# Gated scan and top-2 mixture of experts on one core: one PSUM-bank step in each pump call, and both input transposes of the next expert in one set

## The chip, the cores and the metric

The kernel runs on one core of a Trainium2 chip. The metric is the device time of one execution in microseconds (us). Beside the plain runs there is one profiled execution, whose trace gives the start and length of every instruction on five engines: PE (TensorE matmul, with PEld for its weight loads), DVE (VectorE), ACT (ScalarE), POOL (GpSimd) and SP (SyncE, which only issues DMAs).

## What is computed

The input has 8 groups of 1024 tokens with 256 channels, all float32. There are two layers, each behind a layernorm and with a residual.

```
h    = rmsnorm(layernorm(x)) * gamma
q, kv, a = split(h @ w_qkva.T)                 # 256 channels each
y_t  = sigmoid(a_t) * y_(t-1) + kv_t           # a scan over the 1024 tokens of a group
x    = x + q * y
z    = layernorm(x)
for each token: the two best of 8 experts by softmax(z @ router_w),
    at most 256 tokens of a group per expert (CAP), the gates are the softmax values
expert e: (gelu(z @ w0[e]) * (z @ w1[e])) @ wo[e]     # 256 -> 1368 -> 256
out  = x + sum over the token's experts of gate * expert output
```

## The kernel before, in words

**Blocks.** The 8 groups are worked in four blocks n = 0 to 3 of two groups. The token work (scan layer, router, gates) of a block runs in units u of 512 tokens, four to a block. The expert work of a block is 8 experts e, each with 2 x 256 gathered token rows. An expert's hidden width of 1368 is cut into six sets s = 0 to 5 of 256 columns (the last has 88), so a block has 48 sets and the program has 192. While PE multiplies the experts of block n, the token work of block n+2 is woven between the products.

**A set (`run_set`, L880).** The two-by-two block products are done in Strassen's manner, seven products in place of eight, with sums of weights made on POOL (`row_sums`, `out_sums`) and sums of inputs on DVE. A product is four matmuls of 256 columns. Four products add up one after the other in one bank z, and ACT copies z out after the first, second and third (the snapshots `snap0`, `snap1`, `snap2` at L913, L927, L934). The fourth, `st.mm(z, a22, t4, False)` at L947, may only write z when the third snapshot has been taken. Between these products stand second-layer products of earlier sets (`products()`, with a hand-written list of shares by set: set 1 has none between the third and the fourth z product), and two calls of `pump()`: the first between the third and the fourth z product (L943), the second at the set's end (L961). The engines' queues follow the order in which the program is written (`tc.manual_schedule`): nothing is reordered.

**PSUM.** There are eight banks: y0 to y3 hold the experts' output sums, z0 and z1 alternate as z of a set, `pb` is a third product bank, and `aside` is for everything else. In a set with bank z0, the bank z1 first takes the product `p_a` (L918), which DVE reads soon after; from then until the next set takes it as its z it is free, and is called `spare`. All work that is not an expert product takes its bank from `ps_a` (L69), which goes round the list `side`:

```
side[:] = ["aside", spare]
pump()
side[:] = [spare]
```

A bank is one buffer: the next use of it waits until the last one has been read by ACT or DVE.

**The work between.** A pump call runs the closures that a planner (L1038 to L1062) put into it. The token work is a list of steps in fixed order, each with a weight (`weigh`, L197), and the planner puts steps into call k of 88 until their weights reach an even share of the sum; what doesn't fit goes to call 88 (the block has 96). A step "with a bank" is one in which PE writes a bank for ACT or DVE to read: `h_channels` and `x_channels` (four transposes, L192, then an ACT copy), `gate_a`, `scan` and `mix` (a projection, L257, read by ACT, by the DVE scan, by a DVE multiply), `to_tokens` (transposes L290, a DVE add), `router` (L327), `positions` and `tokens` (L415 and L506). The other steps are DVE work: layernorm moments, row scaling, softmax, one-hot rows, and so on.

**`between()`** (L1092) does the expert's own side work by set: the transposes of the next expert's gathered rows (`input_channels`, L671: two halves k, four transposes each, an ACT copy each) in sets 1 and 3, or in 3 and 4 for the first expert of a block and for the second of block 0; and in sets 2 and 5 the transposes of the previous expert's outputs (`output_rows`, L863, an ACT copy, a DMA to DRAM). In set 1 it runs in front of the fourth z product, in every other set behind it. `column_sums` (DVE, sets 4 and 5) then makes the sums of the next expert's inputs. In set 1 DVE also joins the previous expert's output sums (`join_outputs`).

Of the kernel before, what the change touches and what calls it, by code (L numbers as in the profile page):

```python
# [17 lines left out]
def kernel(  # L18
# [15 lines left out]
    KC = D // P  # L34
# [159 lines left out]
            )  # L194
        nc.scalar.copy(dst[:, k, :], pt)

    def weigh(w, f):  # L197

        f.weight = w
        return f  # L200

    mid_front = []
# [3 lines left out]
    def unit_steps(u, ps):  # L206
# [127 lines left out]
                pl[:, : UT * NE],  # L334
            )

        def each(w, f):
            return [weigh(w, lambda c=c: f(c)) for c in range(2)]

        pause = [weigh(0, lambda: None)]  # L340
        before_mixer = each(12, first_moments) + each(12, first_norm) + pause
        before_mixer += each(3, h_channels)
        mixer = [f for fs in zip(each(5, gate_a), each(13, scan), each(7, mix)) for f in fs]
        mixer += pause + each(7, to_tokens)
        after_mixer = each(12, second_moments) + each(10, second_norm) + pause
        after_mixer += each(3, x_channels)
        after_mixer.append(weigh(3, router))
        return before_mixer, mixer, after_mixer

    def gate_steps(n):  # L350
# [148 lines left out]
        def tokens(gl):  # L499
            tn = v["tn"]  # L500
            ptok = ps_a(f"ptok_{n}_{gl}")
            for q in range(2 * TPG):
                r, j = divmod(q, TPG)
                at = hot.pop((gl, q))
                for hh in range(NH):
                    nc.tensor.matmul(  # L506
                        ptok[:, hh * 2 * NE : (hh + 1) * 2 * NE],
                        lhsT=at[:, hh * P : (hh + 1) * P],
                        rhs=tn[:, r, gl * TPG + j].rearrange("p k e -> p (k e)"),
                        start=(q == 0 and hh == 0), stop=True, skip_group_check=True,  # L510
                    )
            pk = ptok[:, : NH * 2 * NE].rearrange("p (h k e) -> p h k e", h=NH, k=2)
            td = pg.tile([P, NH, NE], FP, tag="td", name=f"td_{n}_{gl}")
            V.tensor_scalar(td, pk[:, :, 0, :], float(P), None, ALU.mult)
            V.tensor_tensor(tok[n][:, gl], td, pk[:, :, 1, :], ALU.add)
# [1 line left out]
        steps = [weigh(12, softmax), weigh(9, softmax_sum)]  # L517
        steps += [weigh(10, lambda r=r, q=q: top(r, q)) for r in range(2) for q in range(2)]
        steps += [weigh(13, lambda q=q: counts(q)) for q in range(2)]
        steps += [weigh(7, positions), weigh(9, places), weigh(9, kept),  # L520
                  weigh(6, output_places), weigh(20, slot_tokens)]
        for gl in range(GB):
            steps += [weigh(13, lambda gl=gl, q=q: one_hot(gl, q)) for q in range(4)]
            steps.append(weigh(6, lambda gl=gl: tokens(gl)))
        return steps

    def combine_steps(n):
# [137 lines left out]
    def input_channels(n, e, k):  # L665

        if k == 0:
            cols[n, e] = pb.tile([P, KC, GB, CAP], FP, tag="xT", name=f"xT_{n}_{e}")
        pt = ps_a(f"px_{n}_{e}_{k}")
        for q in range(UT):  # L670
            nc.tensor.transpose(  # L671
                pt[:, q * P : (q + 1) * P], inputs[n, e][q][:, k * P : (k + 1) * P], ident
            )
        nc.scalar.copy(cols[n, e][:, k, :, :].rearrange("p g s -> p (g s)"), pt)
# [205 lines left out]
    def run_set(j, last, due, pump, between):  # L880


        V, A = nc.vector, nc.scalar
        st = Set(j)
        a11, a12, a22, s1, s2, s3, s4 = st.a
        b11, b21, b22, t1, t2, t3, t4 = st.b
        nm = f"{st.n}_{st.e}_{st.s}"
        z, p_b = bank(f"z{j % 2}", f"z_{nm}"), bank("pb", f"pb_{nm}")
        st.pb = p_b
        st.hid = pb.tile([P, GB, 2, CAP], FP, tag="hid", name=f"hid_{nm}", bufs=3)  # L890
        st.h2 = st.hid.rearrange("p g c s -> p g (c s)")
        zz = st.cut(z)
        work = [f for o in due for f in out_work(o)]
        summed = last and last.s < NS - 1 and not plain(last.n, last.e)
        joined = units[units.index((st.n, st.e)) - 1] if st.s == 1 and j > NS else None
        if joined and plain(*joined):
            joined = None
        if st.s == 1:
            shares = [1, 2, 1, 0, 0]
        elif len(due) > 1:  # L900
            shares = [1, 1, 2, 2, 2]
        elif due and plain(due[0].n, due[0].e):
            shares = [1, 0, 1, 1, 1]
        else:
            shares = [0, 2, 1, 3, 1] if st.s == 2 else [2, 0, 1, 3, 1]

        def products():
            for _ in range(min(len(work), shares.pop(0))):
                work.pop(0)()

        st.mm(z, a11, b11, True)
        snap0 = st.ten("snap", "sn0", 4)
        A.copy(snap0, zz)  # L913
        if last:
            first_gate(last)
        products()
        spare = f"z{1 - j % 2}"
        p_a = bank(spare, f"pa_{nm}")  # L918
        st.mm(p_a, a12, b21, True)
        c11 = st.ten("cg", "c11", 3)  # L920
        V.tensor_tensor(c11, snap0, st.cut(p_a), ALU.add)  # L921
        if last:
            second_gate(last)
        products()
        st.mm(z, s2, t2, False)
        st.snap1 = st.ten("snap", "sn1", 4)
        A.copy(st.snap1, zz)  # L927
        if joined:
            join_outputs(*joined, 0)
        products()  # L930
        st.mm(p_b, s1, t1, True)
        st.mm(z, s3, t3, False)
        snap2 = st.ten("snap", "sn2", 4)
        A.copy(snap2, zz)  # L934
        A.activation(c11, c11, AF.Gelu_apprx_tanh)
        V.tensor_tensor(st.h2[: st.hs, 1, st.wide], snap2, st.cut(p_b), ALU.add)  # L936
        if joined:
            join_outputs(*joined, 1)
        elif summed:
            hid_sums(last, 0)  # L940
        products()
        side[:] = ["aside", spare]
        pump()  # L943
        side[:] = [spare]
        if st.s == 1:
            between()
        st.mm(z, a22, t4, False)  # L947
        V.tensor_tensor(st.h2[: st.hs, 0, st.wide], zz, c11, ALU.mult)  # L948
        if joined:
            join_outputs(*joined, 2)  # L950
        if st.s != 1:
            between()
        side[:] = ["aside"]
        products()
        st.mm(p_b, s4, b22, False)
        first_sum(st)
        if joined:
            hid_sums(last, 0)
        if summed:
            hid_sums(last, 1)  # L960
        pump()  # L961
        return st
# [73 lines left out]
    with tc.manual_schedule():  # L1036
        last, pending, late = None, [], [[] for _ in range(UB)]
        for n in range(NB):  # L1038
# [12 lines left out]
            if n + 1 < NB:  # L1051
                steps = list(token_work[n + 2])
                share = (sum(f.weight for f in steps) + sum(load[: PUMPS - 8])) / (PUMPS - 8)
                done = 0.0
                for k in range(PUMPS - 8):
                    done += load[k]
                    while steps and done + steps[0].weight / 2 <= share * (k + 1):
                        done += steps[0].weight
                        at_pump(k, steps.pop(0))
                for f in steps:  # L1060
                    at_pump(PUMPS - 8, f)
                at_pump(PUMPS - 7, lambda n=n: gather_unit(n + 1, 0))  # L1062
# [12 lines left out]
            def pump():  # L1075
                for f in plan.pop(at[0], []):
                    f()
                j, half = at[0] // 2 + n * NE * NS, at[0] % 2
                e, s = at[0] // (2 * NS), j % NS
                nxt = (n, e + 1) if e + 1 < NE else (n + 1, 0)  # L1080
                later = (n, e + 2) if e + 2 < NE else (n + 1, 1)
                if half == 0:
                    if j == 0:
                        gather_unit(0, 1)
                    if s == NS - 1 and e + 2 != NE and later in units:
                        gather_unit(*later)
                if nxt in units:
                    if s == (4, 5)[1 - half]:
                        column_sums(*nxt, 1 - half)
                at[0] += 1  # L1090

            def between():  # L1092
                q = at[0] // 2
                e, s = q // NS, q % NS
                nxt = (n, e + 1) if e + 1 < NE else (n + 1, 0)

                slots = (3, 4) if nxt[1] == 0 or nxt == units[1] else (1, 3)
                if s in slots and nxt in units:
                    input_channels(*nxt, slots.index(s))
                before = (n, e - 1) if e > 0 else (n - 1, NE - 1)  # L1100
                if s in (2, 5) and before in yts:
                    output_rows(*before, s // 5)
                    if s == 5:
                        yts.pop(before)
# [50 lines left out]
```

## Time and profile before

| | |
|---|---|
| median of 3 runs | 2044.55 us (2042.69 to 2045.44) |
| the profiled execution, own time | 2044.96 us |
| its span, first to last instruction | 2043.1 us |
| PE busy | 1986.1 us (97%), 9352 matmuls |
| PE weight loads busy | 1633.9 us (80%) |
| DVE, POOL, ACT busy | 1360.0, 1236.5, 685.6 us |
| the expert work's first set starts | 140.0 us after the span's start |

The profiled execution lies 0.41 us above the median, and its span 1.9 us below its own time. Matmuls are pipelined: one of 256 columns is listed with some 380 ns, and the next starts 216 ns after it. So an idle time that the profile lists before a matmul begins only when the listed end has passed, and the stream of starts was by then some 165 ns late.

### The profile page before, as it was taken

Reading aid. Unit: us, or ns where it says so; the run is one execution under the profiler, and the core shown is the slowest. Engines: PE = TensorE matmul, PEld = TensorE weight load, DVE = VectorE, ACT = ScalarE, POOL = GpSimd, SP = SyncE. Lnnn points to the kernel's source line nnn. Section 1 sums busy time; section 2 is a strip of 40 time slices with the busy share of each in tenths; the row PEclk is TensorE's granted clock in tenths of the full one; section 3 lists DMA queues with packets and bytes.
Section 4 is the critical chain, followed back from the end, with each engine's and each line's share of the span. In section 5 each row is a group of like instructions: output and inputs, shape, how many; then the busy total and the mean of one; then the engine's idle time right before and its main releaser. Section 6 shows DMA issues by size and latency. Waiting matters only on the chain.

```text
span 2043.1 us, 27788 instructions
## 1 busy us (share of the span) xinstructions
PE 1986.1 (97%) x9352; PEld 1633.9 (80%) x9352; DVE 1360.0 (67%) x2617; ACT 685.6 (34%) x1286; POOL 1236.5 (61%) x1754
## 2 busy tenths in 40 slices
PE   8889999999999999999999999999999999999999
PEld 4557777888888778788888878888888888888887
DVE  4466565676866575768776666677876677666645
ACT  3233333333333233333333333334333333333332
POOL 2327465545656565767665666666756677677557
PEclk9789999999999999999999999999999999999999
DMA  5223333323323334443424343444434343443453
GB/s 175 73 75 98 91 99 93 107 83 102 108 77 108 116 88 132 119 147 109 133 81 117 109 119 93 140 130 120 124 102 114 104 124 110 129 136 107 123 169 96
DMA packets 224077, 228.87 MB, mean 112 GB/s; under 512 B 32448, under 2 KB 215744, under 8 KB 223936
## 3 DMA queue, kind: packets, MB, share of 16 engines
q1 hardware_dynamic: 211104, 193.51, 32.1%
q0 software_dynamic: 12288, 33.57, 5.5%
q8 instruction: 76, 1.25, 0.3%
q14 instruction: 65, 0.53, 0.1%
q10 hardware_dynamic: 544, 0.01, 0.0%
HBM read 185.61 MB, written 41.42 MB: 111 GB/s over the span
## 4 chain that ended last, share of the span: by engine, by line
PE 91%; DVE 4%; POOL 2%; ACT 2%; issue 1%; DMA 1%; SPq 0%; DVEq 0%; ACTq 0%; POOLq 0%
PE z L745 30%; PE acc L797 24%; PE pb L745 15%; PE pa L745 7%; PE pa L257 3%; PE pkv L257 2%; PE pq L257 2%; PE py L777 2%; PE pl L327 1%; PE pt_y L863 1%; PE px L671 1%; PE po L290 1%; ACT sn L934 1%; PE pt_h L192 1%; PE pt_x L192 0%
## 5 line engine op out<-in xcount | busy, mean ns | idle before, releaser
L701 POOL TENSOR_TENSOR sb<-w 128x256 f32<-128x256 f32 x188 | 130.1, 692 | 418.3 <-PE pb L745 417.5
L745 PE MATMUL z<-tb,sb 128*128 128x256 f32 (+1 forms) x1408 | 368.2, 380 | 0.0
L936 DVE TENSOR_TENSOR hid<-sn,pb 128x512 f32<-128x512 f32 x192 | 123.0, 641 | 270.7 <-ACT sn L934 270.7
L745 PEld LDWEIGHTS z<-tb,sb 128*128 128x128 f32 (+1 forms) x1408 | 264.3, 188 | 42.0 <-issue 0.6
L913 ACT COPY sn<-z 128x512 f32<-128x512 f32 x192 | 105.6, 550 | 396.4 <-PE z L745 396.4
L797 PE MATMUL acc<-hid,wo 128*128 128x256 f32 x840 | 222.5, 382 | 0.0
L797 PE MATMUL acc<-tw,so 128*128 128x256 f32 x900 | 218.7, 379 | 0.0
L921 DVE TENSOR_TENSOR c<-sn,pa 128x512 f32<-128x512 f32 x192 | 122.2, 637 | 125.8 <-PE pa L745 123.6
L934 ACT COPY sn<-z 128x512 f32<-128x512 f32 x192 | 105.6, 550 | 277.9 <-PE z L745 277.9
L745 PE MATMUL z<-tb,w 128*128 128x256 f32 (+1 forms) x704 | 187.6, 385 | 9.4 <-ACT sn L934 9.4
L927 ACT COPY sn<-z 128x512 f32<-128x512 f32 x192 | 105.6, 550 | 269.0 <-PE z L745 268.9
L797 PEld LDWEIGHTS acc<-tw,so 128*128 128x128 f32 x900 | 171.0, 190 | 24.2
L745 PE MATMUL z<-xT,w 128*128 128x256 f32 (+1 forms) x704 | 187.9, 386 | 0.0
L745 PE MATMUL pa<-xT,w 128*128 128x256 f32 (+1 forms) x704 | 186.9, 385 | 0.5 <-DVE hid L948 0.4
L745 PE MATMUL pb<-xT,sb 128*128 128x256 f32 (+1 forms) x704 | 184.5, 381 | 0.0
L745 PE MATMUL pb<-tb,sb 128*128 128x256 f32 (+1 forms) x704 | 183.5, 379 | 0.0
L797 PEld LDWEIGHTS acc<-hid,wo 128*128 128x128 f32 x840 | 160.9, 192 | 23.4
L871 DVE TENSOR_TENSOR c<-sn,pb 128x512 f32<-128x512 f32 x192 | 122.7, 639 | 75.1 <-PE pb L745 74.0
L745 PEld LDWEIGHTS z<-tb,w 128*128 128x128 f32 (+1 forms) x704 | 126.7, 187 | 46.8 <-ACT sn L934 17.7
L745 PEld LDWEIGHTS z<-xT,w 128*128 128x128 f32 (+1 forms) x704 | 130.0, 190 | 32.7 <-issue 11.6
L704 POOL TENSOR_TENSOR sb<-w,sb 128x256 f32<-128x256 f32 x188 | 155.2, 825 | 0.0
L658 POOL DMA_INDIRECT xg<-xn,tok x128 | 127.9, 1000 | 39.1 <-issue 31.9
(176 smaller groups left out, 3788.6 us busy)
## 6 DMA issues: line engine op xcount, KB each, us to landing
w<-in_L_ffn_w_kernel_dram SPq DMA_DIRECT2D x320, 256.0 KB
wo<-in_L_ffn_wo_kernel_dram SPq DMA_DIRECT2D x160, 256.0 KB
y<-ot SPq DMA_DIRECT2D x62, 256.0 KB
xt<-in_L_attn_x_dram SPq DMA_DIRECT2D x16, 512.0 KB
x<-xt SPq DMA_DIRECT2D x16, 512.0 KB
xn<-xn SPq DMA_DIRECT2D x16, 512.0 KB
xc<-x SPq DMA_DIRECT2D x16, 512.0 KB
out_dram<-xc SPq DMA_DIRECT2D x12, 512.0 KB
```

The lines of the kernel that those rows point to most:

```text
L257: nc.tensor.matmul(pp, lhsT=wT[:, k, c * P : (c + 1) * P], rhs=t["hT"][:, k, :], start=(k == 0), stop=(k == KC - 1),)
L658: nc.gpsimd.indirect_dma_start(out=xg, out_offset=None, in_=xn_d[n * GB + gl][:, :], in_offset=bass.IndirectOffsetOnAxis(ap=tok[n][:, gl, ...
L701: eng.tensor_tensor(s1, a21, a22, ALU.add)
L704: eng.tensor_tensor(s4, a12, s2, ALU.subtract)
L745: nc.tensor.matmul(ps[:hs, i * CAP : (i + 1) * CAP], lhsT=a[:, i * hs : (i + 1) * hs], rhs=b, start=first and i == 0, stop=True, skip_grou ...
L797: nc.tensor.matmul(ys[n, e, i][:, half * CAP : (half + 1) * CAP], lhsT=lhsT, rhs=rhs, start=fresh, stop=True, skip_group_check=True,)
L871: nc.vector.tensor_tensor(st.c12, st.snap1, st.cut(st.pb), ALU.add)
L913: A.copy(snap0, zz)
L921: V.tensor_tensor(c11, snap0, st.cut(p_a), ALU.add)
L927: A.copy(st.snap1, zz)
L934: A.copy(snap2, zz)
L936: V.tensor_tensor(st.h2[: st.hs, 1, st.wide], snap2, st.cut(p_b), ALU.add)
```

## The change

The planner is told which steps need a bank (`banks`, a second argument of `weigh`), and puts at most one of them into a pump call; when a second one is due, the call is closed, and that step and all behind it go to the next. The weights of these steps become 6 where they were 3 or 5. Both halves of the next expert's input transposes are made in set 1 (the exception keeps sets 3 and 4). `between()` stands in front of the fourth z product in every set. The banks go round differently: the step in the first pump call takes `spare` first, and `between()` takes `aside` first and then `spare`. No instruction is added or removed.

```diff
-    def weigh(w, f):
+    def weigh(w, f, banks=0):
-        f.weight = w
+        f.weight, f.banks = w, banks
...
-        before_mixer += each(3, h_channels)
-        mixer = [f for fs in zip(each(5, gate_a), each(13, scan), each(7, mix)) for f in fs]
-        mixer += pause + each(7, to_tokens)
+        before_mixer += each(6, h_channels, 1)
+        mixer = [f for fs in zip(each(6, gate_a, 1), each(13, scan, 1), each(7, mix, 1)) for f in fs]
+        mixer += pause + each(7, to_tokens, 1)
...
-        after_mixer += each(3, x_channels)
-        after_mixer.append(weigh(3, router))
+        after_mixer += each(6, x_channels, 1)
+        after_mixer.append(weigh(6, router, 1))
...
-        steps += [weigh(7, positions), weigh(9, places), weigh(9, kept),
+        steps += [weigh(7, positions, 1), weigh(9, places), weigh(9, kept),
...
-            steps.append(weigh(6, lambda gl=gl: tokens(gl)))
+            steps.append(weigh(6, lambda gl=gl: tokens(gl), 1))
...
         products()
+        side[:] = [spare, "aside"]
+        pump()
         side[:] = ["aside", spare]
-        pump()
-        side[:] = [spare]
-        if st.s == 1:
-            between()
+        between()
+        side[:] = ["aside"]
         st.mm(z, a22, t4, False)
         V.tensor_tensor(st.h2[: st.hs, 0, st.wide], zz, c11, ALU.mult)
         if joined:
             join_outputs(*joined, 2)
-        if st.s != 1:
-            between()
-        side[:] = ["aside"]
         products()
...
                     done += load[k]
+                    free = 1
                     while steps and done + steps[0].weight / 2 <= share * (k + 1):
+                        free -= steps[0].banks
+                        if free < 0:
+                            break
                         done += steps[0].weight
                         at_pump(k, steps.pop(0))
...
-                slots = (3, 4) if nxt[1] == 0 or nxt == units[1] else (1, 3)
-                if s in slots and nxt in units:
-                    input_channels(*nxt, slots.index(s))
+                slots = (3, 4) if nxt[1] == 0 or nxt == units[1] else (1, 1)
+                if nxt in units:
+                    for k in range(KC):
+                        if s == slots[k]:
+                            input_channels(*nxt, k)
```

## The prediction

> **What bounds the kernel now.** I read the page first: busy times, the clock in slices, the chain that ended last.
>
> ```profile
> PE 1986.1 (97%) x9352; PEld 1633.9 (80%) x9352; DVE 1360.0 (67%) x2617; ACT 685.6 (34%) x1286; POOL 1236.5 (61%) x1754
> ...
> PEclk9789999999999999999999999999999999999999
> ...
> PE 91%; DVE 4%; POOL 2%; ACT 2%; issue 1%; DMA 1%; SPq 0%; DVEq 0%; ACTq 0%; POOLq 0%
> ```
>
> PE carries the chain from end to end. The change adds and removes no matmul, so all that can move is time in which PE stands still or runs slowly. I therefore asked for PE's own waits after 140 us, where the expert sets start; what comes before isn't touched.
>
> ```profile
> PE z L745 <- ACT sn L934: 9.4, 26, 0.7
> PE ptok L506 <- DVE oneh L496: 3.1, 4, 2.1
> PE pt_x L192 <- DVE oT L284: 2.9, 3, 1.1
> PE pt_h L192 <- ACT xnT L195: 2.3, 4, 0.7
> PE po L290 <- ACT xnT L195: 1.6, 3, 0.7
> ...
> PE po L290 <- ACT logits L332: 1.4, 5, 0.3
> PE pt_x L192 <- ACT hT L195: 1.4, 2, 0.7
> ```
>
> Two kinds. The first row is the fourth z product waiting for the third snapshot. Most of the rest are steps with a bank waiting until an earlier step's bank has been read (a transpose into `pt_x` doesn't need `oT`: it needs the bank that the multiply into `oT` was reading). The timelines of PE show one of each, set 1 of an expert and a pump call with four bank steps:
>
> ```profile
> 722.20 1.03 PE L745 MATMUL z<-tb,sb 128*128 128x256 f32 x4
> 723.07 0.60 PE L671 MATMUL px<-ident,xg 128*128 128x128 f32 x4
> 723.96 1.13 PE L745 MATMUL z<-tb,w 128*128 128x256 f32 x4 [0.29 <-ACT sn L934]
> ```
>
> ```profile
> 693.32 1.88 PE L257 MATMUL pq<-hT,wT 128*128 128x512 f32 x4
> 696.26 0.66 PE L192 MATMUL pt_x<-ident,xn 128*128 128x128 f32 x4 [1.07 <-DVE oT L284]
> 697.60 0.66 PE L192 MATMUL pt_h<-ident,h 128*128 128x128 f32 x4 [0.68 <-ACT xnT L195]
> 698.93 1.11 PE L192 MATMUL pt_x<-ident,xn 128*128 128x128 f32 x4 [0.68 <-ACT hT L195]
> 699.84 1.91 PE L745 MATMUL z<-xT,w 128*128 128x256 f32 x4
> ```
>
> The last row is stretched: four matmuls that elsewhere take 1.03 us take 1.91. The windows view (third number from the end: the granted clock) says why.
>
> ```profile
> 695.10:698.50 3.40, 1.41 (x9) 0.83 (x8) 1.07 (x3) 0.80 (x2) 2.77 (x4) 1.00 0.90 266
> 698.50:701.90 3.40, 2.97 (x9) 2.58 (x10) 0.00 (x0) 1.08 (x3) 3.17 (x5) 0.50 0.77 267
> ```
>
> **What the skill says.** The Trainium skill, "Perfetto Trace Analysis", Matmuls, wants independent groups to go round different banks so that emptying one overlaps the next group; the rows above are places where that fails. "PSUM — Partial Sum Buffer", PSUM bank collisions, has a bank guarded as a whole, which is why any reader of it holds the next writer. "TensorE: Matmul & The Clock Gate", Part 1, says that the clock is judged in free-running windows of 3413 ns and goes to half after an idle one. The trace agrees on length (after 140 us, stretches at half clock of 3.41, 3.41, 3.41, 6.83 and 3.41 us, at 316, 699, 712, 801 and 1511 us) but not on "idle"[...]. Four of the five follow calls with several bank steps, the fifth a wait of `ptok`.
>
> **The change, part by part.** A wait costs more than its listed idle time: the start stream is 0.165 us late when idle begins (380 minus 216 ns), and the matmul behind the restart comes 0.10 us late (0.055 for a transpose), as starts in the trace show.
>
> *One bank step in a call.* I worked the planner's loop through by its weights. Before, 25 calls hold 68 bank steps, so 43 steps stand behind another in one call. After, all 55, 55 and 30 bank steps of the three lists find calls of their own, none is left for call 88. In the waits list, rows of that kind (all with L192, L257, L290, L327, L863 waiting) sum to 14.5 us in 27 waits: 14.5 + 27 x 0.22 = **20.4 us gone**. A lone first-call step reads its bank back before the next set's z product wants `spare`: that product comes exactly where a second-call step stood when `aside` was reused, and of the nine cases of that in the trace with one step in each of the two calls none waited. What is late next: a DVE step in front of a bank step in a first call (about 5 calls), 0.5 us in all, from 0 to 3.
>
> *Slow clock.* 20.5 us at half speed lost 10.2. Without the piles I expect one new stretch, 1.7: **8.5 gone**; ends 3 and 10.2.
>
> *Set 1.* It has 27 experts with transposes there. Before, 21 wait 0.29 + 0.165 + 0.104 = 0.56 us, three (with a step in the call) 0.13: 12.2. With eight transposes (8 x 0.109 = 0.87) in front, the snapshot, ready 0.89 after the third product, leaves 0.02 + 0.10. That holds where the first call has no bank step: 14 x 0.125 = 1.75. In the other 13 the step takes `spare`, the first half `aside`, and the second half needs `spare` again: it waits for the step's reader. Say T is the end of the third z product. From the set at 723.07: ACT copies the snapshot at T + 0.25, has gelu to do, and its next copy ends at T + 1.84; so five calls with an ACT reader (one `hT`, one `xnT`, three transposes of block 3) wait from T + 0.87 to T + 1.9: 1.07 with restart. DVE does two 0.6 us operations first and begins the step's at T + 2.07 (set at 782.41): an add of 0.69 (`to_tokens`, two calls) 2.0 us, a multiply behind a projection of 1.72 (one call) 0.7, a scan of 1.25 (three) 1.3, a router (two) 0.15. Sum 5.35 + 4.0 + 0.7 + 3.9 + 0.3 = 14.3. Set 1 after: 16.0, **3.8 worse**. Behind the waiting transposes stand the fourth z product and all of PE; DVE and ACT have slack there.
>
> *`tokens`.* 3.1 us of listed idle in 4 waits is 4.9 with lateness and restarts; the calls with the last one-hot rows and `tokens` together fall from three to two, priced by the like ones of before at 1.0 and 0.4: **3.4 gone**; from 0 to 4.9.
>
> *`between()` in front, `aside` first.* The z product behind an output transpose no longer waits for its ACT copy (14 times 0.077 by the starts): **1.1 gone**. The other moved transposes change places with a product, at no cost as long as their rows are there: the gather of the next block's first expert landed 0.8 us (block 1) and 1.0 us (block 3) before its transposes, which now come 1.0 earlier: 0.5 lost, from 0 to 1. No DMA or POOL instruction is moved past another by more than a pump call. One set 1 without input transposes gets a shorter step: 0.4 lost. Softmax, whose table load holds ACT for 1.28 us, now falls into a set 1 with a router and delays the second half's copy and so the next z product: 0.6 lost.
>
> Sum: 20.4 + 8.5 - 3.8 + 3.4 + 1.1 - 0.5 - 0.5 - 0.4 - 0.6 = 27.6. The profiled execution took 2044.96, so 2017.4; it lay 0.41 above the median, so **2017**.
>
> **Rivals.**
> 1. *The waits are only thinned* (chance 0.20): a lone step finds its input not ready, because list order and DVE's backlog now bite. For it: DVE is 67% busy, and `ptok` waited for it. Against it: lone steps in the trace hardly ever waited. Half of 20.4 and 4 of the clock back: 2031.
> 2. *Set 1 blocks* (0.05): the second half waits behind the step in 13 sets for 2 us or more, and each such hole (with 16 transposes, little else) brings a half-clock window of 1.7: 13 x 3.7 = 48.1, against 20.4 + 10.2 + 3.4 + 1.1 + 12.2 - 1.75 - 2.0 = 43.5 of gains: 4.6 slower, 2049. It decides from 3.35 us per place; my prices are 0.15 to 2.0, mean 1.1, for which the trace's ACT and DVE orders speak.
> 3. *Set 1 costs little* (0.14): the readers are done earlier than I have it, so that a quarter of the 14.3 is left, and no clock stretch: 2017.4 - 10.7 - 1.7 = 2005.
> 4. *The change doesn't separate the steps* (0.04): if steps piled up in call 88, time would stay. The worked plan leaves none over; then 2044.
>
> **Numbers.** The main case has 0.57, with 2010 to 2024 for its own range. About 0.2% (4 us) is what a measurement of this kernel can tell from no change. Taking in rival 1 and most of 3, and the ends above: 2005 to 2033. Faster 0.91, same 0.04, slower 0.05.
>
> **What would show it.** Right: rows of L192, L257, L290 and L327 nearly gone from PE's waits; `z L745 <- ACT sn L934` down from 9.4 us to that of the sets without transposes, some 3.5; new rows `px L671` waiting for ACT `at`/`hT`/`xnT` or DVE `xt`, `y`, `oT` of about 11 us listed (14.3 less 13 x 0.22); the clock at 1.00 in nearly every window after 140 us. Wrong: bank steps still waiting one by one, `px` rows over 25 us, or the next set's `z<-xT,w` waiting for DVE.

## The result, and the profile after

The changed kernel takes 2024.0 us (median of 5 runs, 2023.14 to 2026.28), the kernel before 2042.69 in the same session (2035.5 to 2045.44). The ratio is 0.9914, interval 0.9893 to 0.9934. The profiled execution after took 2023.14 us with a span of 2021.3, against 2044.96 and 2043.1 before: 21.8 us less in both.

The page of the changed kernel, busy times, the clock in slices and the chain that ended last:

```profile
PE 1968.5 (97%) x9352; PEld 1629.9 (81%) x9352; DVE 1365.1 (68%) x2617; ACT 682.1 (34%) x1286; POOL 1231.8 (61%) x1754
...
PEclk9779999999999999999999999999999999999999
...
PE 88%; DVE 5%; POOL 2%; issue 2%; ACT 1%; DMA 1%; SPq 0%; DVEq 0%; ACTq 0%; POOLq 0%
```

The same 9352 matmuls are listed with 17.6 us less busy time. I take these to be matmuls that ran at half clock, and listed ends that were stretched over a late start; the two were not split. The page's share of PE hardly tells; its waits after 140 us do (line, released by; us in total, times, longest):

```profile
PE px L671 <- DVE xt L296: 3.6, 2, 1.8
PE z L745 <- ACT sn L913: 3.5, 1, 3.5
PE z L745 <- ACT sn L934: 3.5, 6, 0.7
PE px L671 <- DVE y L277: 3.1, 3, 1.1
PE px L671 <- ACT places L621: 2.6, 3, 0.9
PE acc L797 <- POOL so L727: 1.6, 2, 1.3
...
PE pa L745 <- DVE hid L948: 1.5, 5, 0.4
PE px L671 <- ACT xnT L195: 0.9, 1, 0.9
PE px L671 <- ACT hT L195: 0.9, 1, 0.9
PE pb L745 <- DVE hid L936: 0.7, 2, 0.4
PE px L671 <- DVE oT L284: 0.5, 1, 0.5
```

No row of `pt_h`, `pt_x`, `po` or `pl` is left: a bank step no longer waits for another one in its own call. The wait for the third snapshot (`sn L934`) fell from 9.4 us in 26 waits to 3.5 in 6. In their place stand rows of `px`, 11.6 us in 11 waits: the second half of the input transposes waiting for the reader of the step that took `spare` first. The timeline of PE shows the dearest of them, a `to_tokens` step (`po`) in the first call of set 1:

```profile
706.70 0.60 PE L290 MATMUL po<-ident,oT 128*128 128x128 f32 x4
707.14 0.60 PE L671 MATMUL px<-ident,xg 128*128 128x128 f32 x4
709.52 0.66 PE L671 MATMUL px<-ident,xg 128*128 128x128 f32 x4 [1.78 <-DVE xt L296]
710.01 1.03 PE L745 MATMUL z<-tb,w 128*128 128x256 f32 x4
```

The step's matmuls end, the first half goes into `aside` at once, the second half stands 1.94 us (709.52 less the 707.58 at which it was due), and the fourth z product and everything else of PE stand behind it. Without a step in that call, eight transposes run on into the z product with 0.02 us of delay.

One row was not on my list at all: 3.5 us for the *first* snapshot, `sn L913`. PE's timeline at the place, and then ACT's:

```profile
413.72 1.03 PE L797 MATMUL acc<-hid,wo 128*128 128x256 f32 x4
418.27 1.10 PE L745 MATMUL z<-tb,sb 128*128 128x256 f32 x4 [3.53 <-ACT sn L913]
```

```profile
410.68 1.28 ACT L372 ACT_TABLE_LOAD   x1
417.35 0.31 ACT L372 ACTIVATE raw<-raw 128x128 f32<-128x128 f32 x1 [5.38 <-DVE raw L371]
417.56 0.57 ACT L913 COPY sn<-z 128x512 f32<-128x512 f32 x1
```

ACT stood 5.38 us at the softmax's exponential, waiting for a DVE subtraction (L371), with the next set's first snapshot queued behind. DVE's timeline shows what the subtraction stood behind:

```profile
412.28 0.69 DVE L855 TENSOR_TENSOR yT<-yT,acc 128x512 f32<-128x512 f32 x1
...
415.95 0.68 DVE L296 TENSOR_TENSOR xt<-po,xt 128x512 f32<-128x512 f32 x1
416.55 0.27 DVE L370 TENSOR_REDUCE red<-logits 128x16 f32<-128x128 f32 x1
416.85 0.46 DVE L371 TENSOR_TENSOR raw<-logits,red 128x128 f32<-128x128 f32 x1
```

DVE was late because the softmax now fell into the second call of a set 1, behind the joins of the previous expert's sums (L855), the sums of hidden rows, and a `to_tokens` addition (L296). Before, the softmax stood in sets 0 and 5, and the exponential never waited for DVE.

The granted clock, by its own record, was 1.00 from 143.4 us to 0.6 us before the end; before, the five stretches at half clock lay there, and the slow clock of the start-up lasted until 145.6 us.

### The profile page after: what moved, and what is told of

It is laid out like the page before. It is cut to its first block, busy times and chain, and to the rows that moved or that the text cites. A ratio compares the mean times of both kernels' runs of the same rounds, so it can differ in the third digit from the quotient of the medians.

```text
span 2021.3 us, 27735 instructions
## 1 busy us (share of the span) xinstructions
PE 1968.5 (97%) x9352; PEld 1629.9 (81%) x9352; DVE 1365.1 (68%) x2617; ACT 682.1 (34%) x1286; POOL 1231.8 (61%) x1754
## 4 chain that ended last, share of the span: by engine, by line
PE 88%; DVE 5%; POOL 2%; issue 2%; ACT 1%; DMA 1%; SPq 0%; DVEq 0%; ACTq 0%; POOLq 0%
PE z L745 29%; PE acc L797 23%; PE pb L745 14%; PE pa L745 7%; PE pa L257 3%; PE pq L257 2%; PE pkv L257 2%; PE py L777 2%; PE pl L327 1%; PE px L671 1%; PE pt_y L863 1%; DVE y L277 1%; PE po L290 1%; PE pt_h L192 1%; ACT sn L934 1%
## 5 line engine op out<-in xcount | busy, mean ns | idle before, releaser
L913 ACT COPY sn<-z 128x512 f32<-128x512 f32 x192 | 105.6, 550 | 432.5 <-PE z L745 432.5
L934 ACT COPY sn<-z 128x512 f32<-128x512 f32 x192 | 105.6, 550 | 278.3 <-PE z L745 278.3
L948 DVE TENSOR_TENSOR hid<-z,c 128x512 f32<-128x512 f32 x192 | 123.0, 641 | 73.9 <-PE z L745 73.3
```

## The experiments

For each trace I also give the time from the start of block 0's first set to that of block 3's first set, taken from the timeline: 1450.8 us before, 1427.6 after. It is free of the end, but not quite of the start: the slow clock of the start-up reaches into block 0, by 5.6 us before and by 2.8 after. By the starts of the matmuls (how much later each starts than the pace of full clock allows) that cost 2.8 and 1.4 us. The first four variants ran on another chip, on which the kernel before took some 25 us more (2067.94). Their traces have it in block 3: 473.6 to 476.7 us from its first set to PE's last matmul, against 448.0 before and 448.8 after. No trace of the kernel before or of the changed one was taken there. So only ratios to the kernel before and blocks 0 to 2 are compared across the chips.

**The planner's part alone**, against the changed kernel:

```diff
-        side[:] = [spare, "aside"]
+        side[:] = ["aside", spare]
         pump()
-        side[:] = ["aside", spare]
-        between()
-        side[:] = ["aside"]
+        side[:] = [spare]
+        if st.s == 1:
+            between()
         st.mm(z, a22, t4, False)
...
+        if st.s != 1:
+            between()
+        side[:] = ["aside"]
...
-                slots = (3, 4) if nxt[1] == 0 or nxt == units[1] else (1, 1)
+                slots = (3, 4) if nxt[1] == 0 or nxt == units[1] else (1, 3)
```

> Only the planner's part of the change (one bank step in a call, the new weights); the order of the banks, between() and the input transposes in sets 1 and 3 are as before. Theory (the gain is that bank steps no longer stand one behind another, and that the half-clock stretches go with them; the moved transposes cost about as much as they give): before less 20 (piles) less up to 10 (clock) less 3 (tokens) plus about 6 for new waits at the softmax and behind DVE; in set 1 the 13 calls with a step hide the snapshot at no cost and 14 sets wait 0.56 us as before. About 2017 us, from 2013 to 2022, so faster than the changed kernel by some 5. Rival (the moved transposes carry the gain): 2035 or more.

Measured: 2046.64 us, ratio 0.9895 (0.9878 to 0.9912). Blocks 0 to 2 took 1425.8 us: 25.0 less than before, 1.8 less than with the whole change. The planner's part carries the gain; the rival is out. Which of its two edits does it, the limit of one bank step or the new weights, was not tried apart. The ratios of this variant and of the whole change don't differ beyond their intervals; in blocks 0 to 2 the 5 us expected became 1.8. This variant ran 12.5 us of block 0 at half clock and the changed kernel 2.8; by the starts of the matmuls that cost it 4.3 us more, so without it this variant would have been some 6 us ahead, an estimate. PE's waits of this variant from 140 to 1566 us:

```profile
PE z L745 <- ACT sn L934: 5.4, 14, 0.7
PE z L745 <- ACT sn L913: 3.5, 1, 3.5
```

The third snapshot is waited for in 14 sets again, and the softmax's wait came here too, this time with the clock: the windows view (third number from the end)

```profile
412.20:415.60 3.40, 0.95 (x5) 0.50 (x3) 3.30 (x6) 0.00 (x0) 3.30 (x6) 0.99 0.00 0
415.60:419.00 3.40, 2.31 (x6) 1.89 (x7) 1.30 (x3) 2.87 (x5) 0.00 (x0) 0.50 0.47 159
419.00:422.40 3.40, 3.40 (x10) 2.68 (x9) 0.22 (x1) 0.42 (x1) 0.00 (x0) 0.50 0.00 0
```

shows one window filled by the wait and then two at half clock. In the changed kernel the same wait straddled two windows and cost no clock, though PE's listed busy time was under half of each:

```profile
413.10:416.50 3.40, 1.65 (x8) 1.11 (x6) 3.33 (x5) 0.00 (x0) 3.32 (x6) 1.00 0.00 0
416.50:419.90 3.40, 1.63 (x8) 1.48 (x9) 1.46 (x4) 2.53 (x4) 0.66 (x2) 1.00 0.45 159
```

**The other part alone**, against the kernel before; its planner stays:

```diff
-        side[:] = ["aside", spare]
+        side[:] = [spare, "aside"]
         pump()
-        side[:] = [spare]
-        if st.s == 1:
-            between()
+        side[:] = ["aside", spare]
+        between()
+        side[:] = ["aside"]
         st.mm(z, a22, t4, False)
...
-                slots = (3, 4) if nxt[1] == 0 or nxt == units[1] else (1, 3)
+                slots = (3, 4) if nxt[1] == 0 or nxt == units[1] else (1, 1)
```

> Only the other part of the change (both transposes in set 1, between() in front of the fourth z product, spare first in the first call); the planner is as before. Theory: the piles and their half-clock stretches stay; set 1 gains 0.44 us in some 21 sets and loses 0.7 to 1.2 in six: 3 to 4 us, and 1 us behind the output transposes: about 2038 us, from 2033 to 2042, with 15 us or more of the clock at half after 140 us. Rival (this part carries the gain): 2030 or less.

Measured: 2067.46 us, ratio 1.0000 (0.9988 to 1.0011): 0.5 us less in the medians where 4 were expected, a miss in time. In blocks 0 to 2 it is 1447.4, 3.4 us less than before, as expected. The start came 1.0 us later; where the rest went isn't shown, since block 3 has no like on that chip. The piles stayed, as PE's waits from 140 to 1588 us show (the largest rows):

```profile
PE pt_x L192 <- DVE oT L284: 2.9, 3, 1.1
PE ptok L506 <- DVE oneh L496: 2.7, 3, 2.1
PE z L745 <- ACT sn L934: 2.2, 3, 0.7
```

The slow clock stayed too: four stretches from 215 to 1512 us, 20.5 us together, as much as before. Three of them lie at calls where the kernel before had one (699, 801 and 1511 us there). The stretches at 316 and 712 us did not come, though their piles stood, and one came at 215 us, behind a pile of four steps that stood in the kernel before too, in the same order and with the same waits. There it had fallen across two windows of the clock; here it filled one.

**The first call of set 1 kept free of bank steps**, against the changed kernel:

```diff
-                    free = 1
+                    free = int(k % (2 * NS) != 2 or k > 84)
...
-                    at_pump(8 + 2 * i, f)
+                    at_pump(9 + 2 * i, f)
```

> The changed kernel, with no bank step planned into the first call of set 1 where both input transposes follow; in block 3 the steps of the last expert are put one call later for the same reason. Theory (the second transposes wait for the step that took spare): the 11 waits of px, 13.3 us of late starts in the changed kernel's trace, go; each of those sets is left with 0.12: about 12 us off the changed kernel, 2012, from 2008 to 2016, and no px row in PE's waits. Rival (the steps that are pushed on crowd the other calls and bring as many waits): within 4 us of the changed kernel.

Measured: 2037.33 us, ratio 0.9856 (0.9835 to 0.9877). Against the changed kernel's 0.9914, measured on the other chip, that is 0.0058, 12 us, as expected; blocks 0 to 2 took 1417.8, 9.8 less. Counted by the starts in set 1, the lateness fell from 15.9 us in the changed kernel to 3.5, with 2.9 of the difference in block 3. No `px` row is left in PE's waits from 140 to 1558 us, which begin so:

```profile
PE z L745 <- ACT sn L913: 5.0, 2, 3.5
PE z L745 <- ACT sn L934: 1.8, 3, 0.7
PE pa L745 <- DVE hid L948: 1.1, 4, 0.4
```

The softmax's wait has moved from block 0 to blocks 1 and 2. Freed of the step, the moved transposes beat the planner's part alone by 8.0 us in blocks 0 to 2. Of these, 4.3 are what half clock cost the other variant in block 0 beyond this one; some 4 us are left, although this variant waited 1.6 us longer at the softmax. So the moved transposes do give.

**The softmax in three calls**, against the changed kernel, with the exponential in a step `softmax_exp` of its own:

```diff
-        steps = [weigh(12, softmax), weigh(9, softmax_sum)]
+        steps = [weigh(9, softmax, 1), weigh(3, softmax_exp, 1), weigh(9, softmax_sum, 1)]
```

> The changed kernel, with the softmax's subtraction, its exponential (ACT, with a table load of 1.28 us) and its sum in three calls. Theory (in block 0 the exponential sits on ACT behind DVE's queue, and the first snapshot of the next set behind it: a wait of 3.7 us; in block 2 the same way 0.4): 4 us off the changed kernel, about 2020, and no wait of z for the first snapshot. Rival (the table load itself holds ACT long enough to delay a snapshot wherever it stands): no more than 1 us off.

Measured: 2050.96 us, ratio 0.9921 (0.9905 to 0.9938); blocks 0 to 2 took 1428.7, 1.1 more than the changed kernel. No wait for the first snapshot is left, as the theory had it, but there is no gain: the 4 us expected did not come. Setting three steps apart pushed the later gate steps on, and the trace has longer waits after them: PE for POOL's `so` (start 2.65 us late at 458 us, and a half-clock window behind it), for DVE's `hid` (0.9 us in block 0, two of 1.2 to 1.3 in block 1). That the pushed steps made these waits is argued from their places, not shown.

**The changed kernel again**, with no edit.

> The changed kernel itself, once more, so that the other variants can be set beside it on one chip. Theory (the waits follow from the order of the queues, so they are the same ones): the same ratio to the kernel before, 0.991; px waits of some 13.3 us of late starts, no half-clock stretch in blocks 0 to 2. Rival (the gain hangs on where the clock's windows fall): a ratio off by 0.004 or more.

Measured: 2023.73 us, ratio 0.9914 (0.9900 to 0.9927). Blocks 0 to 2: 1427.6; each wait listed above agrees within 0.1 us; no half-clock stretch between 150 us and the end.

**The kernel before again**, with no edit.

> The kernel before itself, with a profile, beside the others. Theory: PE's waits in blocks 0 to 2 as in its first profile, within 0.5 us for each row; half-clock stretches again right behind calls with several bank steps, some four to six windows, though not all at the same calls, since the windows run free; and in block 3 the long waits at the last expert's third set that the variants showed on this chip. Rival (the stretches have nothing to do with the piles): other places, or none.

Measured: 2044.51 us, one run. Blocks 0 to 2: 1450.8, and PE's waits of before again, row by row. The half-clock stretches came at the same five calls, within 0.5 us, where I had expected some to change place. But the clock's windows of this trace happened to lie within 0.4 us of those of the first, so it hardly tested that. The long waits of block 3 weren't there, on this chip; what makes them on the other one wasn't tried.

**The free call, and the exponential one step later**, against the variant with the free call:

```diff
             tt(raw, L, over_e(red), ALU.subtract)
-            nc.scalar.activation(raw, raw, AF.Exp)
...
             raw, red = v["raw"], v["red"]
+            nc.scalar.activation(raw, raw, AF.Exp)
             V.tensor_reduce(red, raw, AX.X, ALU.add)
```

> The variant with the first call of set 1 kept free, and the softmax's exponential moved out of the softmax step to the head of the step that sums it, one or two calls later; weights and number of bank steps stay. Theory (ACT takes its work in order; the exponential, waiting for DVE, holds the first snapshot of the next set): the waits of z for the first snapshot, 3.7 us in block 1 and 1.6 in block 2, go, and DVE waits some 1.6 us for the exponential where it has slack: 4 us off that variant, ratio to before about 0.9835. Rival (the table load delays a snapshot anyway): within 1 us of that variant.

Measured: 2007.38 us, ratio 0.9835 (0.9820 to 0.9849), as expected, and faster than both kernels. Blocks 0 to 2: 1412.4, 5.4 less than with the free call alone. Blocks 1 and 2, where the waits for the first snapshot had stood, give 4.8 of it. Block 0 gives only 0.5, although it lost 1.4 us less to the start-up's slow clock, which here ended before the first set. All of PE's waits after 140 us:

```profile
PE z L745 <- ACT sn L934: 3.5, 6, 0.7
PE pa L745 <- DVE hid L948: 2.1, 5, 0.9
PE py L777 <- DVE hid L878: 1.6, 2, 1.0
PE pb L745 <- DVE hid L936: 1.6, 3, 0.8
PE ptok L506 <- DVE oneh L496: 0.4, 1, 0.4
PE z L745 <- POOL sb L702: 0.3, 1, 0.3
PE acc L797 <- POOL so L727: 0.3, 1, 0.3
```

The three table loads of 1.28 us are still there, and no row for the first snapshot is left: what had hurt was not the load but ACT waiting with a snapshot queued behind.

## Why the prediction was right, and where it was off

The direction and the range held; the size was 27.6 us, and 21.8 came in the profiles and 18.7 in the medians. The median of 2024.0 lies at the slow end of the main case's own range. Of the difference, 3.1 lies between profile and median: the first profile stood 0.4 above the median of the three runs then shown, but 2.3 above that of five, and the profile after 0.9 below its median. The other 5.8 us are steps of the sum, and two of its errors cancelled in part, which is luck. Counted by the starts of the matmuls, the clock gave 11.5 us where 8.5 were forecast; the first set came 0.6 later; so 10.9 are left for the waits, where the other terms come to 19.1. Step by step:

- **One bank step in a call, 20.4:** as worked out. Every row of that kind is gone, and the variant with the planner alone shows that it is this part.
- **Slow clock, 8.5:** the five stretches had cost 10.1, as worked out, and all of it is gone. No new stretch came in the changed kernel; the one that I had set against it did come in two variants, behind a long wait inside one window. Another 1.4 came from the start-up's slow clock, whose end lies after 140 us and which the working left out; why it ended earlier was not tried. That the piles caused the stretches is backed by the run with the piles kept, where three of the five came at the same calls and each of the four lies at a pile or at the `tokens` call, and by the traces without piles, whose stretches in blocks 0 to 2, after the start-up, came behind another long wait or not at all. Which pile brings one depends on where the windows fall, as the pile at 215 us shows.
- **Set 1, 3.8 worse:** as priced. The late starts of `px` were 1.03 us behind ACT readers, 1.19 to 1.25 behind scans, 0.66 behind the multiply and 1.94 behind the additions, against 1.07, 1.3, 0.7 and 2.0; they sum to 13.3 us, and with 0.6 of restarts to 13.9, against 14.3. The two routers priced at 0.15 cost 0.1 together. All of set 1 was late by 15.9 us, against the 16.0 forecast. The run with the call kept free gave 12 us back, which shows the cause.
- **`tokens`, 3.4:** the two remaining calls stood as priced, 0.4 us of listed idle.
- **The softmax, 0.6 lost: the step that failed in size.** I looked at the table load, and only in sets 1 with a router. The loss was 3.7 us of late start in block 0, and not from the table load but from the exponential's wait for DVE, with the snapshot behind it on ACT. My working named what is queued behind PE's waiting instructions, and not what is queued behind ACT's.
- **A DVE step in front of a bank step, 0.5 (0 to 3):** too narrow in kind. The new waits for DVE are `pa` for `hid` (1.1 us more listed idle), `pb` for `hid` (0.7), and for the sum that frees `spare` itself (0.5); POOL's `so` came 1.0 us later in one place. With restarts and lateness that is some 5 us for which the sum had 0.5. What makes each of them was not tried apart.
- **The gather, 0.5 lost:** no `px` waited for its rows, so this did not come.

The terms of 1.1 and 0.4 were not traced singly. Of the 8.2 us that the waits fell short, the steps above explain some 7; the rest is open.

Of the rivals, the blocked set 1 was the right mechanism at a third of the price from which it decides: 13.9 / 13 = 1.07 us per place against 3.35. The rival of thinned waits was wrong as told: lone bank steps found their inputs ready, but for the two last `tokens` calls.

## What to carry to other kernels

When engines run in program order, and the next borrower of a bank stands right behind the last, PE waits until the last one's reader has come round. So count the borrowers between two uses of a bank, and look at what the reader's engine has in front. Two borrowers in one place can be a wait wherever they meet: the change cured it in the planner and made it anew between the planner's step and its own transposes. After moving work, look at the queue behind every instruction that may have to wait, on ACT as well as on PE.

## What the runs showed of the hardware

The half clock follows the work within one window of 3.41 us, and PE need not be idle for a whole window. I counted each matmul from its start by its columns, at the 216 ns that 256 columns take at full clock. In the nine traces, from 145 us to 20 us before the end, all 23 full-clock windows with less than 0.38 of a window's length of such work were followed by half clock, and none with 0.39 or more was. The two windows nearest to the edge in the first trace of before are those at 709 us (0.37, slow behind it) and 586 us (0.39, not slow); both hold a router's 16 matmuls of 8 columns, which this count takes with 7 ns each.

A wait of 3.5 us therefore cost its own length where it straddled two windows (418 us in the changed kernel: 0.45 of work in each), and some 2.6 us more where it filled one (412 us in the planner's part alone: 0.24). There two windows at half clock followed, and PE was still waiting for the first 1.1 us of them. Where the windows fall is not fixed: their first boundary lay from 0.04 to 3.16 us after the span's start in the nine traces. That the wait straddled two windows in both traces of the changed kernel is therefore luck, worth some 2.6 us.
